# An adaLN block with attention and a mixture of experts: sums of the shared weights prepared in the last batch, the second norm's centring on another engine, other buffers for the experts

## The chip, the cores and the metric

The kernel runs on one core of one Trainium2 chip. The metric is device time in microseconds (us) of one execution. The core's engines are PE (TensorE, matrix products), DVE (VectorE), ACT (ScalarE), POOL (GpSimd) and SP (SyncE, which here issues nearly all DMA transfers). Each engine works through its own list of instructions in order and waits on semaphores that other engines or transfers raise.

## The reference, cut to what matters

All data are float32. x has 4 batches of 512 tokens of width 512. The six modulation rows come from c.

```python
mod = (silu(c) @ wmod).reshape(4, 6, 1, -1)
sa, ca, ga, sb, cb, gb = (mod[:, i] for i in range(6))      # ga, gb kept away from 0
h = layernorm(x) * (1 + ca) + sa
x = x + ga * attention(h)          # 16 heads of 128, causal softmax, q/k/v/o with biases
h = layernorm(x) * (1 + cb) + sb
x = x + gb * ffn(h)
```

ffn is a mixture of 8 experts (SwiGLU, 352 wide, the best 2 of 8 by a softmax over `gate_weight`) plus a shared SwiGLU MLP of width 704 over all tokens:

```python
g = silu(x @ w_gate[e].T) * (x @ w_up[e].T)          # routed, weighted by the two best scores
y = sum_e cw[:, e] * (g @ w_down[e].T)
y = y + (silu(x @ sw_gate.T) * (x @ sw_up.T)) @ sw_down.T
```

## The kernel before

**Products of seven.** Large matrix products are cut into 2 x 2 quadrants and made with seven products instead of eight (`seven`, L483). Each operand then needs seven slots: its four quadrants, partly overwritten, and sums of them. `sums_of_a` (L466) and `sums_of_b` (L473) make the sums in four operations of one engine, over the slots of one tile. For the q, k, v and o weights, the sums made in batch 0 are stored to DRAM tensors (`sums`, L141) and loaded in the later batches.

**Attention.** Batch b (B = 4) has four groups of four heads; G counts the sixteen groups, u the heads of a group (loop at L1018). For a head, `first_half` makes the scores: PE products into `ps`, DVE mask L756 and maximum L758, ACT's exponential L760. `second_half` makes the rest a head later: DVE's reciprocal L764, ACT's scaling of prob in four pieces L767, PE's transposes `ppt` L777, the copies to `probT` by DVE (L785) or ACT (L787), PE's `po` L791 and ACT's `oS` L798. The sums of oS are made on POOL (L468 to L471). The projections of other groups fill in between: `weave_at` takes steps of the fill (next_k, next_v, next_o, with products w_k L612, w_v L660, w_o L697) by the tables PLANS, OPENING and LAST, written by hand. `second_norm(b - 1)` (L916) is a side generator, stepped at fixed spots of batch b's first two groups.

**The second norm** is `normed(b, 2)` (L207). For each of four blocks of 128 tokens, DVE multiplies the attention output by ga (L217) and POOL adds x (L218). DVE takes mean and variance (L223, L224), L228 adds epsilon, and ACT makes rstd by Ln and Exp (L229, L230). After a yield, DVE makes xh = (x - mean) * rstd (L233) for each block, multiplies by 1 + cb (L242), and POOL adds sb (L243). PE turns xh (`pln`, L251); then `route` (L274) computes the experts' scores, picks two (`hit`, L351) and counts tokens ahead of each (`prk`, L357 and L360), from which come the slots to which POOL scatters the tokens (L380).

**The shared weights.** `wshr` holds, one after the other, five chunks of gate and up weights (ws, each four quadrants of 2 x 128 columns), the tail wst, and the down weights sdn (four quadrants of 3 x 256). At the second head of the last group, (G, u) = (15, 1), the pool of attention's weights is closed and the tiles ws[0] to ws[4] and wst are opened (L1059). wst, ws[0] and ws[1] are loaded there; at (15, 3) DVE makes the sums of those two (L1083). After attention SP loads h2s of batches 0 and 1 (L1470), the other three ws and sdn. POOL makes the sums of h2s_0, ws[2] to ws[4] and sdn, and DVE those of h2s_1 (L1495 to L1500).

**After attention.** `shared(0)` makes the hidden layer of the shared MLP for batches 0 and 1, five chunks of seven products each (`shared_hidden` L1169, matmul w_s L1177, DVE L1189 to L1207, SiLU on ACT L1190 and L1194, the product into hid L1218), then the down products (w_d L1250) with the sums of hid on DVE or POOL (L1235). `shared_tail` (L1148, pst L1152) makes the narrow tail chunk. Between its steps runs `slots_found` (L1502): the second norm of batch 3, its route and the plan of tiles. Then come 39 tiles of 128 tokens for the experts (loop at L1534) with two buffers each for the weights wgu and wdn; at tile 4 h2s of batches 2 and 3 are loaded. Last comes `half2`: shared(2) for batches 2 and 3, woven (L1577 to L1579) with `combined`, which fetches the experts' outputs by indirect DMA, scales and adds them (L1459 to L1465) and writes the output. In `half2` POOL makes the sums of h2s_2 and DVE those of h2s_3.

**Memory and order.** The pool `moe` (L1114) opens when attention's pool closes, and takes over its memory: gb_bc, sdn, then wgu[0], wgu[1], wdn[0], wdn[1], then two h2s tiles. A tile there waits for the former users of the memory under it. The order on PE, DVE, ACT and SP is as the program writes it (`manual_schedule`); POOL's order is chosen by a scheduler from its dependencies.

Of the kernel before, what the change touches and what calls it, by code (L numbers as in the profile page):

```python
# [8 lines left out]
F32 = mybir.dt.float32  # L9
# [5 lines left out]
P = 128  # L15
# [15 lines left out]
SQ = 4 * 2 * P  # L31
FK = 3
FL = FS // 2 - 2 * P
SW = NSC * SQ + NC * P + 4 * FK * HW
EGU = 2 * NC * F
TOPK = 2
# [11 lines left out]
def adaln_block_kernel(  # L48
# [29 lines left out]
    def bank(tag, name):  # L78
        if tag in ("ps", "pt"):
            return psum.tile([P, 512], F32, tag=tag, name=name)  # L80
        bufs = {"w": 3, "po": 1}[tag]
        return psum2.tile([P, 512], F32, tag=tag, bufs=bufs, name=name)
# [30 lines left out]
    for i in range(NT):  # L113
# [29 lines left out]
        "wk": dram.tile([H // 2, P, 5 * 2 * DH], F32, name="sums_k"),  # L143
        "wv": dram.tile([NG, P, 5 * 4 * DH], F32, name="sums_v"),
        "wo": dram.tile([NG, P, 2 * 6 * HW], F32, name="sums_o"),
    }


# [58 lines left out]
    def normed(b, n, fine=(1,)):  # L207


        if n == 1:  # L210
            src = xh = late["first"]
        else:
            src = xres[b]
            xh = late["x"]
            rows = late["mod"]
            for t in range(NTB):
                nc.vector.tensor_mul(src[:, t, :], src[:, t, :], ga_bc)  # L217
                nc.gpsimd.tensor_add(src[:, t, :], src[:, t, :], xh[:, t, :])  # L218
                yield
        mv = small.tile([P, NTB, 2], F32, tag="mv", name=f"mv_{n}_{b}")  # L220
        for t in range(NTB):
            st = small.tile([P, 6], F32, tag="st", name=f"st_{n}_{b}_{t}")
            nc.vector.bn_stats(st, src[:, t, :])  # L223
            nc.vector.bn_aggr(mv[:, t, :], st)  # L224
            if t in fine:
                yield
        rstd = small.tile([P, NTB], F32, tag="rstd", name=f"rstd_{n}_{b}")
        nc.vector.tensor_scalar_add(rstd, mv[:, :, 1], EPS)  # L228
        nc.scalar.activation(rstd, rstd, AF.Ln)  # L229
        nc.scalar.activation(rstd, rstd, AF.Exp, scale=-0.5)  # L230
        yield
        for t in range(NTB):
            nc.vector.tensor_scalar(  # L233
                xh[:, t, :],
                src[:, t, :],
                mv[:, t, 0:1],
                rstd[:, t : t + 1],
                op0=ALU.subtract,
                op1=ALU.mult,
            )  # L240
            if n == 2:
                nc.vector.tensor_mul(xh[:, t, :], xh[:, t, :], rows[0])  # L242
                nc.gpsimd.tensor_add(xh[:, t, :], xh[:, t, :], rows[1])  # L243
            if t in fine:
                yield
        late[b] = xh
# [27 lines left out]
    def route(b, xh):  # L274
# [77 lines left out]
        for t in range(NTB):  # L352
            k = b * NTB + t
            nc.vector.tensor_add(seen[:, k + 1, :], seen[:, k, :], hit[:, t, :])
        yield
        pr = bank("pt", f"prk_{b}")[:, : NTB * NE]
        nc.tensor.matmul(  # L357
            pr, lhsT=before, rhs=hit.rearrange("p t e -> p (t e)"), start=True, stop=False
# [114 lines left out]
    def sums_of_b(eng, w):  # L473

        eng.tensor_sub(w[:, 4], w[:, 3], w[:, 1])
        eng.tensor_sub(w[:, 1], w[:, 1], w[:, 0])
        eng.tensor_sub(w[:, 5], w[:, 3], w[:, 1])
        eng.tensor_sub(w[:, 6], w[:, 5], w[:, 2])

    att = left.enter_context(tc.tile_pool(name="att", bufs=2))  # L480
    wts = right.enter_context(tc.tile_pool(name="wts", bufs=2, side="right"))
# [434 lines left out]
    def second_norm(b):  # L916
# [2 lines left out]
        yield  # L919
        yield from route(b, late[b])  # L920


    def by_turns(*gens):

# [77 lines left out]
    with tc.manual_schedule(engines={ENG.PE, ENG.DVE, ENG.Activation, ENG.SP}):  # L1002
# [11 lines left out]
        weave(queries(0), 8 * SEVEN, fill, 18)  # L1014
        drain(fill)

        pending = None
        for G in range(NGB):  # L1018
            b, g = divmod(G, NG)

# [12 lines left out]
            for u in range(GH):  # L1033
                prob = att.tile([P, 10 * P], F32, tag="prob", name=f"prob_{G}_{u}")
                parts = [first_half(G, u, prob)]
                if pending is not None:
                    parts.append(second_half(*pending))
                pending = (G, u, prob)


                spots = ()
                if g == 0 and b > 0 and u > 0:
                    if u == 1:
                        second = side = second_norm(b - 1)
# [12 lines left out]
                next(parts[0])  # L1057
                weave_at(main, plans[u], fill, side if spots else None, spots)
                if (G, u) == (NGB - 1, 1):  # L1059
                    right.close()  # L1060
                    shp = right.enter_context(
                        tc.tile_pool(name="shared", bufs=1, side="right")
                    )
                    ws = [
                        shp.tile([P, 7, 2, P], F32, tag=f"ws{k}", name=f"ws{k}")
                        for k in range(NSC)
                    ]
                    wst = shp.tile([P, NC, P], F32, name="wst")
                    nc.sync.dma_start(
                        out=wst.rearrange("p c n -> p (c n)"),  # L1070
                        in_=wshr[:, NSC * SQ : NSC * SQ + NC * P],
                    )

                    def load_ws(k):
                        nc.sync.dma_start(
                            out=ws[k][:, :4].rearrange("p q c n -> p (q c n)"),
                            in_=wshr[:, k * SQ : (k + 1) * SQ],
                        )

                    load_ws(0)  # L1080
                    load_ws(1)
                if (G, u) == (NGB - 1, 3):
                    sums_of_a(nc.vector, ws[0])  # L1083
                    sums_of_a(nc.vector, ws[1])
                if g == 3 and u == 3 and b + 1 < B:

                    long = in_order(second_half(*pending), next_v(G + 1))
                    weave(queries(b + 1), 8 * SEVEN, long, 4 + SEVEN)
                    pending = None

                if b + 1 < B:
                    if (g, u) == (2, 0):
                        load_first(b + 1)
                if (g, u) == (0, 1):
                    wos[G] = load_wo(b, 0)
                if (g, u) == (0, 2 if b > 0 else 1):
                    open_out(b)
                if (g, u) == (3, 2):
                    load_for_second(b)

                k, n = GH * G + u - 1, NROW // P // NFILL
                if 0 <= k < NFILL:
                    nc.sync.dma_start(
                        out=xs[k * n * P : (k + 1) * n * P, :].rearrange(
                            "(p n) (c w) -> p (n c) w", p=P, w=P
                        ),
                        in_=nothing.unsqueeze(1).to_broadcast([P, n * NC, P]),
                    )
# [9 lines left out]
    h2s, hids = {}, {}  # L1118
    phase = []

    wgu = [moe.tile([P, EGU], F32, tag=f"wgu{j}", bufs=1, name=f"wgu{j}") for j in range(2)]
    wdn = [moe.tile([P, EW - EGU], F32, tag=f"wdn{j}", bufs=1, name=f"wdn{j}") for j in range(2)]

    def load_h2(b):
        h2s[b] = moe.tile([P, 7, 2, HW], F32, tag="h2", name=f"h2s_{b}")
        nc.sync.dma_start(
            out=h2s[b][:, :4].rearrange("p q c n -> p (q c n)"),
            in_=h2[b].rearrange("p q c n -> p (q c n)"),
        )

    def flat_of(a):
        return a.rearrange("p q c n -> p (q c n)")
# [336 lines left out]
    with tc.manual_schedule(engines={ENG.PE, ENG.DVE, ENG.Activation, ENG.SP}):  # L1469
        load_h2(0)  # L1470
        load_h2(1)
        for k in range(2, NSC):
            load_ws(k)
        nc.sync.dma_start(
            out=flat_of(sdn[:, :4]), in_=wshr[:, NSC * SQ + NC * P :]
        )
        spread(gb_bc, GB)

        def load_xr(b, pool, tag):
# [15 lines left out]
        sums_of_b(nc.gpsimd, h2s[0])  # L1495
        shared_tail(1)
        sums_of_b(nc.vector, h2s[1])
        for k in range(2, NSC):
            sums_of_a(nc.gpsimd, ws[k])
        sums_of_b(nc.gpsimd, sdn)  # L1500

        def slots_found():  # L1502
            yield from in_order(normed(B - 1, 2, (0, 1, 2)))
# [30 lines left out]
        for i in range(NT + 1):  # L1534
# [15 lines left out]
            if i == 4:  # L1550
                load_h2(2)
                load_h2(3)


        open_phase("half2")
# [2 lines left out]
        load_xr(2, moe, "xr0")  # L1558
        load_xr(0, moe, "xr1")
        shared_tail(2)  # L1560
        sums_of_b(nc.gpsimd, h2s[2])
        shared_tail(3)
        sums_of_b(nc.vector, h2s[3])
        for m in range(4):
            fetch(m, order[m])

# [8 lines left out]

        main, fill = shared(2), combined()
        weave(main, 4, iter(()), 0)  # L1577
        weave(main, NSEV - 4, fill, 6 * NTB)
        weave(main, 2 * SEVEN + 1, fill, 2 * NTB)  # L1579
        drain(main)  # L1580
        drain(fill)
        parts.close()
# [111 lines left out]
```

## Time and profile before

| what | us |
| --- | --- |
| median of 3 runs (lowest, highest) | 1825.65 (1824.71, 1828.13) |
| the profiled execution | 1824.61 |
| its span, first to last instruction | 1822.9 |
| PE busy in the span | 1735.1 |
| DVE, ACT, POOL busy | 897.9, 551.0, 616.8 |
| attention ends (last w_o product done) | 1248 |
| shared(0) ends, tiles begin | 1381 |
| tiles end, half2 begins | 1701 |
| last matmul done | 1811.5 |

The profiled execution is one run; its span leaves 1.7 us of its time outside. In a timeline, a row is a run of like instructions: start, duration, engine, line, operation, operands (out<-in), shape, count; brackets at the end hold the idle time of that engine just before and the instruction that ended it. The granted clock is the share of full speed that TensorE's throttle allowed; 1 is full speed, 0.5 half. PE is busy except for some 88 us, 25 of them before 45 us and after 1811 us, while the first data come in and the last go out.

### The profile page before, as it was taken

How to read it: one execution, taken by the hardware profiler on the slowest of the kernel's cores; microseconds unless marked ns; L12 is line 12 of the kernel's file. 1: busy time of each engine (PE TensorE's matmuls, PEld its weight loads, DVE VectorE, ACT ScalarE, POOL GpSimd, SP SyncE). 2: the span in 40 equal slices, each digit the busy share in tenths (PEclk: the TensorE clock that was granted, in tenths of full speed). 3: DMA queues.
4: the chain of work that ended last, by engine and by line, in shares of the span. 5: the costliest groups of instructions: out<-in, count | busy, mean ns of one | idle time of the engine just before them, and what ended most of it. 6: DMA issues, size and time to landing. Idle time of an engine off the chain costs nothing.

```text
span 1822.9 us, 21901 instructions
## 1 busy us (share of the span) xinstructions
PE 1735.1 (95%) x7637; PEld 1321.2 (72%) x7637; DVE 897.9 (49%) x1884; ACT 551.0 (30%) x1325; POOL 616.8 (34%) x702
## 2 busy tenths in 40 slices
PE   6999999998999999899999899998899999999997
PEld 4767777786887788688788678875686556556685
DVE  4554454457545555654555655444673111211486
ACT  1034444214445412544430444441300111111220
POOL 6334662305243303352320425336341000000575
PEclk9999999999999999999999999999999999999999
DMA  6569899645343333442343243225042656453442
GB/s 247 177 199 294 267 305 312 197 160 193 107 138 113 116 127 113 159 143 88 122 142 108 104 121 127 81 68 203 24 170 88 238 174 220 167 192 132 147 143 75
DMA packets 145007, 287.25 MB, mean 158 GB/s; under 512 B 8177, under 2 KB 86513, under 8 KB 138241
## 3 DMA queue, kind: packets, MB, share of 16 engines
q1 hardware_dynamic: 139776, 269.07, 44.2%
q0 software_dynamic: 5120, 16.78, 2.8%
q8 instruction: 61, 1.00, 0.2%
q14 instruction: 50, 0.40, 0.1%
HBM read 247.38 MB, written 89.69 MB: 185 GB/s over the span
## 4 chain that ended last, share of the span: by engine, by line
PE 77%; DVE 8%; POOL 5%; DMA 4%; ACT 3%; issue 2%; SPq 0%; POOLq 0%; DVEq 0%; ACTq 0%
PE w_v L660 10%; PE w_o L697 10%; PE w_q L574 10%; PE w_k L612 7%; PE ps L749 6%; PE po L791 6%; PE pyt L1419 5%; PE pgt L1392 5%; PE put L1392 5%; PE w_s L1177 3%; PE w_d L1250 3%; PE ppt L777 3%; ACT prob L767 1%; DVE xh L242 1%; PE pxt L1379 1%
## 5 line engine op out<-in xcount | busy, mean ns | idle before, releaser
L760 ACT ACTIVATE prob<-ps,nmax 128x128 f32<-128x128 f32 (+3 forms) x256 | 134.2, 525 | 362.0 <-DVE nmax L758 362.0
L612 PE MATMUL w_k<-h,wk 128*128 128x256 f32 x896 | 222.6, 387 | 4.5 <-ACT p_k L624 2.7
L660 PE MATMUL w_v<-wv,h 128*128 128x256 f32 x896 | 206.1, 380 | 3.0 <-DVE kT L627 1.8
L697 PE MATMUL w_o<-wo,oS 128*128 128x256 f32 x896 | 209.0, 380 | 0.0
L574 PE MATMUL w_q<-h,wq 128*128 128x256 f32 x896 | 203.6, 382 | 1.4 <-DVE qT L600 1.4
L574 PEld LDWEIGHTS w_q<-h,wq 128*128 128x128 f32 x896 | 170.1, 192 | 27.7 <-issue 3.4
L660 PEld LDWEIGHTS w_v<-wv,h 128*128 128x128 f32 x896 | 167.6, 190 | 24.7 <-DVE kT L627 2.2
L612 PEld LDWEIGHTS w_k<-h,wk 128*128 128x128 f32 x896 | 165.8, 195 | 26.8 <-ACT p_k L624 5.8
L697 PEld LDWEIGHTS w_o<-wo,oS 128*128 128x128 f32 x896 | 164.9, 191 | 21.0 <-issue 1.4
L749 PE MATMUL ps<-kT,qT 128*128 128x128 f32 (+3 forms) x512 | 173.5, 440 | 1.7 <-ACT prob L760 1.4
L791 PE MATMUL po<-probT,v 128*128 128x512 f32 (+3 forms) x512 | 150.9, 436 | 11.4 <-DVE probT L785 11.4
L791 PEld LDWEIGHTS po<-probT,v 128*128 128x128 f32 x512 | 95.2, 190 | 68.6 <-issue 28.9
L777 PEld LDWEIGHTS ppt<-ident,prob 128*128 128x128 f32 x640 | 82.9, 142 | 81.9 <-issue 35.9
L767 ACT ACTIVATE prob<-prob,rsum 128x128 f32<-128x128 f32 (+3 forms) x256 | 122.8, 551 | 61.2 <-DVE rsum L764 61.2
L710 POOL TENSOR_TENSOR xres<-xres,p_o 128x512 f32<-128x512 f32 x48 | 60.9, 1269 | 231.0 <-DVE xres L710 137.1
L1177 PE MATMUL w_s<-h2s,ws 128*128 128x256 f32 x560 | 127.6, 386 | 8.8 <-DVE wgu L1207 3.0
L758 DVE TENSOR_REDUCE nmax<-ps 128x1 f32<-128x128 f32 (+3 forms) x256 | 125.8, 491 | 8.8
L1177 PEld LDWEIGHTS w_s<-h2s,ws 128*128 128x128 f32 x560 | 106.1, 192 | 28.4 <-DVE wgu L1207 3.6
L777 PE MATMUL ppt<-ident,prob 128*128 128x128 f32 x640 | 109.2, 278 | 14.9 <-ACT prob L767 12.3
L1419 PE MATMUL pyt<-wdn,hTt 128*128 128x512 f32 (+1 forms) x234 | 107.0, 593 | 0.6 <-ACT yt L1427 0.6
L756 DVE TENSOR_TENSOR ps<-ps,cmask 128x128 f32<-128x128 f32 x256 | 75.0, 293 | 59.9 <-PE ps L749 51.5
L1402 DVE TENSOR_TENSOR ht<-tsg,put 128x352 f32<-128x352 f32 x39 | 20.3, 521 | 170.4 <-PE put L1392 165.7
(270 smaller groups left out, 2433.9 us busy)
## 6 DMA issues: line engine op xcount, KB each, us to landing
wgu<-in_wexp_dram SPq DMA_DIRECT2D x39, 1408.0 KB
xs<-nothing SPq DMA_DIRECT2D x15, 2304.0 KB, 15.6
wdn<-in_wexp_dram SPq DMA_DIRECT2D x39, 768.0 KB, 4.7
wo<-sums_o SPq DMA_DIRECT2D x12, 1536.0 KB, 8.3
wq<-sums_q SPq DMA_DIRECT2D x24, 640.0 KB, 4.6
wk<-sums_k SPq DMA_DIRECT2D x24, 640.0 KB, 4.7
wv<-sums_v SPq DMA_DIRECT2D x12, 1280.0 KB, 7.6
xt<-xs SPq DMA_DIRECT2D x39, 256.0 KB, 3.6
```

What stands on the lines that cost most here:

```text
L574: nc.tensor.matmul(dst, lhsT=w[:, sa, c, :], rhs=h7[b][:, sb_, c, :], start=c == 0, stop=c == 1,)
L612: nc.tensor.matmul(dst, lhsT=w[:, sa, c, :], rhs=h7[b][:, sb_, c, :], start=c == 0, stop=c == 1,)
L660: nc.tensor.matmul(dst[:, t2 * HW : (t2 + 1) * HW], lhsT=h7[b][:, sb_, c, t2 * P : (t2 + 1) * P], rhs=w[:, sa, c, :], start=t2 == 0 and c ...
L697: nc.tensor.matmul(dst[:, t2 * HW : (t2 + 1) * HW], lhsT=oSs[hp][:, sa, t2 * P : (t2 + 1) * P], rhs=w[:, hp, sb_, :], start=t2 == 0 and hp ...
L749: nc.tensor.matmul(ps[:, :n], lhsT=qT[:, q0 : q0 + P], rhs=kT[:, u % 2, :n], start=True, stop=True,)
L760: nc.scalar.activation(blk, ps[:, :n], AF.Exp, bias=nmax, accum_out=rsum[:, i : i + 1])
L767: nc.scalar.mul(blk, blk, rsum[:, k : k + 1])
L777: nc.tensor.transpose(pt[:, at : at + P], prob[:, QO[i] + j * P : QO[i] + (j + 1) * P], ident,)
L791: nc.tensor.matmul(po[:, j * P :], lhsT=v()[:, j, u * DH : (u + 1) * DH], rhs=probT[:, KO[j] : KO[j] + (NTB - j) * P], start=(j == 0), sto ...
L1177: nc.tensor.matmul(dst[:, n * HW : (n + 1) * HW], lhsT=ws[k][:, sa, c, :], rhs=h2s[b + n][:, sb_, c, :], start=(n == 0 and c == 0), stop=( ...
L1392: nc.tensor.matmul(ps[:, :F], lhsT=xT[:, c, :], rhs=wgu[i % 2][:, at : at + F], start=(c == 0), stop=(c == NC - 1),)
L1419: nc.tensor.matmul(py, lhsT=hT_t[:fn, k, :], rhs=wdn[i % 2][:fn, k * D : (k + 1) * D], start=(k == 0), stop=(k == len(FCH) - 1),)
```

## The change

1. A generator `shared_sums` is stepped after each of the first twelve heads of the last batch's groups 0 to 2. It loads one chunk of ws into a buffer of the former wq weights, has POOL make its sums, and at its next step stores all seven slots to a new DRAM tensor, five times; then the same for sdn in four pieces of 64 columns. The host lays sdn out by these pieces.
2. At (15, 1) all five ws are loaded from there, whole, and after attention the whole of sdn. The sums at (15, 3) and those of ws and sdn after attention are gone.
3. In the second norm, of all four batches, ACT makes xh as Identity(x * rstd + less), and a new DVE operation behind Exp makes less = -mean * rstd.
4. In `route` of the last batch there is one more yield ahead of prk.
5. In `moe`, wdn comes first, then both h2s tiles, then wgu.
6. Of the sums of h2s_2 and h2s_3, three each are made by POOL at tile 8, the fourth by POOL after the shared tails; DVE makes none of them.
7. The weave of half2 is cut differently: four steps alone, 29 with 24 steps of the combination, five alone, 12 with 8 (before: 4 alone, 31 with 24, 15 with 8).

```diff
+    "ws": dram.tile([NSC, P, 7, 2, P], F32, name="sums_s"),
+    "sdn": dram.tile([P, 7, FK, HW], F32, name="sums_d"),
...
         nc.scalar.activation(rstd, rstd, AF.Exp, scale=-0.5)
+        if n == 2:
+            less = small.tile([P, NTB], F32, tag="less", name=f"less_{n}_{b}")
+            nc.vector.scalar_tensor_tensor(
+                less, mv[:, :, 0], -1.0, rstd, op0=ALU.mult, op1=ALU.mult
+            )
         yield
         for t in range(NTB):
-            nc.vector.tensor_scalar(
-                xh[:, t, :], src[:, t, :], mv[:, t, 0:1], rstd[:, t : t + 1],
-                op0=ALU.subtract, op1=ALU.mult,
-            )
-            if n == 2:
+            if n == 1:
+                nc.vector.tensor_scalar(...)
+            else:
+                nc.scalar.activation(
+                    xh[:, t, :], src[:, t, :], AF.Identity,
+                    bias=less[:, t : t + 1], scale=rstd[:, t : t + 1],
+                )
                 nc.vector.tensor_mul(xh[:, t, :], xh[:, t, :], rows[0])
                 nc.gpsimd.tensor_add(xh[:, t, :], xh[:, t, :], rows[1])
...
         yield
+        if b == B - 1:
+            yield
         pr = bank("pt", f"prk_{b}")[:, : NTB * NE]
...
+    def shared_sums():
+        n = HW // ND
+        for k in range(NSC):
+            w = wts.tile([P, 7, 2, P], F32, tag="wq", name=f"ws_sums_{k}")
+            nc.sync.dma_start(
+                out=w[:, :4].rearrange("p q c n -> p (q c n)"),
+                in_=wshr[:, k * SQ : (k + 1) * SQ],
+            )
+            sums_of_a(nc.gpsimd, w)
+            yield
+            nc.sync.dma_start(out=sums["ws"][k], in_=w)
+        for k in range(ND):
...
+            sums_of_b(nc.gpsimd, w.rearrange("p (q c n) -> p q c n", q=7, c=FK))
+            yield
+            dst = sums["sdn"].rearrange("p q c n -> p (q c) n")
+            nc.sync.dma_start(out=dst[:, :, k * n : (k + 1) * n], in_=w.rearrange("p (q n) -> p q n", n=n))
+        yield
...
-                    load_ws(0)
-                    load_ws(1)
-                if (G, u) == (NGB - 1, 3):
-                    sums_of_a(nc.vector, ws[0])
-                    sums_of_a(nc.vector, ws[1])
+                    for k in range(NSC):
+                        nc.sync.dma_start(out=ws[k], in_=sums["ws"][k])
...
+                if b == B - 1 and g < 3:
+                    next(prepare, None)
...
+    wdn = [moe.tile([P, EW - EGU], F32, tag=f"wdn{j}", bufs=1, name=f"wdn{j}") for j in range(2)]
+    for b in range(half):
+        h2s[b] = moe.tile([P, 7, 2, HW], F32, tag="h2", name=f"h2s_{b}")
     wgu = [moe.tile([P, EGU], F32, tag=f"wgu{j}", bufs=1, name=f"wgu{j}") for j in range(2)]
-    wdn = [moe.tile([P, EW - EGU], F32, tag=f"wdn{j}", bufs=1, name=f"wdn{j}") for j in range(2)]
...
-        for k in range(2, NSC):
-            load_ws(k)
-        nc.sync.dma_start(out=flat_of(sdn[:, :4]), in_=wshr[:, NSC * SQ + NC * P :])
+        nc.sync.dma_start(out=sdn, in_=sums["sdn"])
...
-        for k in range(2, NSC):
-            sums_of_a(nc.gpsimd, ws[k])
-        sums_of_b(nc.gpsimd, sdn)
...
+            if i == 8:
+                most_of_b(nc.gpsimd, h2s[2])
+                most_of_b(nc.gpsimd, h2s[3])
...
-        sums_of_b(nc.gpsimd, h2s[2])
         shared_tail(3)
-        sums_of_b(nc.vector, h2s[3])
+        rest_of_b(nc.gpsimd, h2s[2])
+        rest_of_b(nc.gpsimd, h2s[3])
...
-        weave(main, NSEV - 4, fill, 6 * NTB)
-        weave(main, 2 * SEVEN + 1, fill, 2 * NTB)
+        weave(main, NSEV - 6, fill, 6 * NTB)
+        weave(main, 5, iter(()), 0)
+        weave(main, 2 * SEVEN - 2, fill, 2 * NTB)
```

`most_of_b` makes slots 4, 5 and 6 of `sums_of_b` (with slot 5 from slots 4 and 0), `rest_of_b` the new slot 1.

More of the change, by code (lines that the diff above doesn't have):

```diff
@@ L33 @@
 FL = FS // 2 - 2 * P
+ND = 4
 SW = NSC * SQ + NC * P + 4 * FK * HW
@@ L230, in normed @@
         nc.scalar.activation(rstd, rstd, AF.Exp, scale=-0.5)
+        if n == 2:
[3 more added lines that the diff above has]
+            )
         yield
         for t in range(NTB):
[L233 to L239, printed above, removed]
-            )
-            if n == 2:
+            if n == 1:
+                nc.vector.tensor_scalar(
+                    xh[:, t, :],
+                    src[:, t, :],
+                    mv[:, t, 0:1],
+                    rstd[:, t : t + 1],
+                    op0=ALU.subtract,
+                    op1=ALU.mult,
+                )
+            else:
+                nc.scalar.activation(
+                    xh[:, t, :],
+                    src[:, t, :],
+                    AF.Identity,
+                    bias=less[:, t : t + 1],
+                    scale=rstd[:, t : t + 1],
+                )
                 nc.vector.tensor_mul(xh[:, t, :], xh[:, t, :], rows[0])
@@ L478, in sums_of_b, with most_of_b, rest_of_b @@
         eng.tensor_sub(w[:, 6], w[:, 5], w[:, 2])
+    def most_of_b(eng, w):
+        eng.tensor_sub(w[:, 4], w[:, 3], w[:, 1])
+        eng.tensor_add(w[:, 5], w[:, 4], w[:, 0])
+        eng.tensor_sub(w[:, 6], w[:, 5], w[:, 2])
+    def rest_of_b(eng, w):
+        eng.tensor_sub(w[:, 1], w[:, 1], w[:, 0])
     att = left.enter_context(tc.tile_pool(name="att", bufs=2))
@@ L920, in second_norm @@
         yield from route(b, late[b])
+    def shared_sums():
[5 more added lines that the diff above has]
+                in_=wshr[:, k * SQ : (k + 1) * SQ],
+            )
+            sums_of_a(nc.gpsimd, w)
+            yield
+            nc.sync.dma_start(out=sums["ws"][k], in_=w)
+        for k in range(ND):
+            w = wts.tile([P, 7 * 2 * P], F32, tag="wq", name=f"sdn_sums_{k}")
+            at = NSC * SQ + NC * P + k * 4 * FK * n
+            nc.sync.dma_start(
+                out=w[:, : 4 * FK * n], in_=wshr[:, at : at + 4 * FK * n]
+            )
+            w = w[:, : 7 * FK * n]
+            sums_of_b(nc.gpsimd, w.rearrange("p (q c n) -> p q c n", q=7, c=FK))
[3 more added lines that the diff above has]
+        yield
     def by_turns(*gens):
@@ L1015, in adaln_block_kernel @@
         drain(fill)
-        pending = None
+        pending, prepare = None, shared_sums()
         for G in range(NGB):
@@ L1072, in adaln_block_kernel @@
                     )
[L1074 to L1078, printed above, removed]
-                    load_ws(0)
-                    load_ws(1)
-                if (G, u) == (NGB - 1, 3):
-                    sums_of_a(nc.vector, ws[0])
-                    sums_of_a(nc.vector, ws[1])
+                    for k in range(NSC):
+                        nc.sync.dma_start(out=ws[k], in_=sums["ws"][k])
                 if g == 3 and u == 3 and b + 1 < B:
@@ L1119, in adaln_block_kernel @@
     phase = []
+    wdn = [moe.tile([P, EW - EGU], F32, tag=f"wdn{j}", bufs=1, name=f"wdn{j}") for j in range(2)]
+    for b in range(half):
+        h2s[b] = moe.tile([P, 7, 2, HW], F32, tag="h2", name=f"h2s_{b}")
     wgu = [moe.tile([P, EGU], F32, tag=f"wgu{j}", bufs=1, name=f"wgu{j}") for j in range(2)]
-    wdn = [moe.tile([P, EW - EGU], F32, tag=f"wdn{j}", bufs=1, name=f"wdn{j}") for j in range(2)]
     def load_h2(b):
-        h2s[b] = moe.tile([P, 7, 2, HW], F32, tag="h2", name=f"h2s_{b}")
+        if b not in h2s:
+            h2s[b] = moe.tile([P, 7, 2, HW], F32, tag="h2", name=f"h2s_{b}")
         nc.sync.dma_start(
@@ L1471, in adaln_block_kernel @@
         load_h2(1)
-        for k in range(2, NSC):
-            load_ws(k)
-        nc.sync.dma_start(
-            out=flat_of(sdn[:, :4]), in_=wshr[:, NSC * SQ + NC * P :]
-        )
+        nc.sync.dma_start(out=sdn, in_=sums["sdn"])
         spread(gb_bc, GB)
@@ L1628, in downs_by_quadrant @@
                 q[k, c, p : p + n] = w[n0 : n0 + n].reshape(n, 2, HW)
-        return q.transpose(2, 0, 3, 1, 4).reshape(P, 4 * FK * HW)
+        q = q.transpose(2, 0, 3, 1, 4).reshape(P, 4 * FK, ND, HW // ND)
+        return q.transpose(0, 2, 1, 3).reshape(P, 4 * FK * HW)
     wk_h = a["attn_Wk"].reshape(D, H, DH)
```

## The prediction

> **What bounds the kernel now.** The page's first part comes first: PE is busy for nearly the whole span, so only what stops PE, or slows it, moves the end.
>
> ```profile
> PE 1735.1 (95%) x7637; PEld 1321.2 (72%) x7637; DVE 897.9 (49%) x1884; ACT 551.0 (30%) x1325; POOL 616.8 (34%) x702
> ```
>
> The list of PE's waits over the span then says what stops it (microseconds in total, times, longest):
>
> ```profile
> PE ppt L777 <- ACT prob L767: 12.3, 18, 2.1
> PE po L791 <- DVE probT L785: 11.4, 8, 3.0
> PE pst L1152 <- DMA h2s<-h: 5.4, 1, 5.4
> ```
>
> To see where these waits lie I read PE's timeline, first at the end of attention and in shared(0); the brackets hold the idle time ahead of a row and its releaser:
>
> ```profile
> 1248.07 3.60 PE L1152 MATMUL pst<-h2s,wst 128*128 128x512 f32 x8
> 1257.08 5.06 PE L1152 MATMUL pst<-h2s,wst 128*128 128x512 f32 x8 [5.41 <-DMA h2s<-h]
> ...
> 1281.57 1.99 PE L1177 MATMUL w_s<-h2s,ws 128*128 128x256 f32 x8 [3.03 <-DVE wgu L1207]
> ...
> 1323.82 0.41 PE L357 MATMUL prk<-hit,before 128*128 128x32 f32 x2 [2.61 <-DVE hit L351]
> ```
>
> The same eight matmuls take 3.60 without a wait and 5.06 after one: the idle time costs a stretch at half clock too (granted clock 0.76 from 1255 to 1262). SP's and POOL's timelines there say why:
>
> ```profile
> 1228.34 23.95 SPq L1126 DMA_DIRECT2D h2s<-h  x2
> ```
>
> ```profile
> 1278.74 1.26 POOL L218 TENSOR_TENSOR xres<-xres,xh 128x512 f32<-128x512 f32 x1
> ```
>
> One row holds both h2s loads: the first went out at 1228.34, the second 23.6 us later, since its buffer had u_o, p_o and xres of the last output product as former users. POOL sums ws and sdn from 1259 on and comes to the norm's add at 1278.74; DVE's bn_stats waits 3.61 for it, and L1207, for which PE waits, is queued behind bn_stats.
>
> The third place is the second norm of batch 0 inside batch 1's attention (batches 1 and 2 repeat it at 738 and 1038 to 0.1 us). DVE, ACT, then PE:
>
> ```profile
> 436.80 0.17 DVE L228 TENSOR_SCALAR rstd<-mv 128x4 f32<-128x4 f32 x1
> ...
> 437.81 0.55 DVE L785 COPY probT<-ppt 128x384 f32<-128x384 f32 x1
> 438.96 0.55 DVE L233 TENSOR_SCALAR xh<-xres,mv,rstd 128x512 f32<-128x512 f32 x1 [0.61 <-ACT rstd L230]
> ```
>
> ```profile
> 438.72 0.21 ACT L230 ACTIVATE rstd<-rstd 128x4 f32<-128x4 f32 x1
> ```
>
> ```profile
> 438.41 0.92 PE L791 MATMUL po<-probT,v 128*128 128x256 f32 x4 [1.54 <-DVE probT L785]
> ...
> 443.35 0.73 PE L777 MATMUL ppt<-ident,prob 128*128 128x128 f32 x2 [2.14 <-ACT prob L767]
> ...
> 448.49 0.33 PE L251 MATMUL pln<-ident,xh 128*128 128x128 f32 x1 [0.82 <-POOL xh L243]
> ```
>
> While ACT loads two tables and makes rstd (to 438.93), DVE does three operations of attention (the mask at 436.88, nmax at 437.20, the copy to probT at 437.81); the last of them frees PE at 438.41.
>
> The last place is half2, where DVE is behind:
>
> ```profile
> 1775.80 2.00 PE L1250 MATMUL w_d<-sdn,hid 128*128 128x256 f32 x8 [2.21 <-DVE hid L1218]
> ...
> 1787.82 2.87 PE L1250 MATMUL w_d<-sdn,hid 128*128 128x256 f32 x12 [1.69 <-DVE h2s L1310]
> ```
>
> **A, end of attention and shared(0): −15.5.** With wdn and the two h2s tiles laid out first, the second h2s load follows the first at once (about 1228.9) and lands near 1245, before PE wants it at 1251.7. That removes 5.41, the half clock (5.06 − 3.60 = 1.46) and some 0.26 of matmul tail that a stop exposes: 7.1. The eight DVE sums of ws (1229.8 to 1233.0) go; probT L785 stood behind them and PE waited 0.33, then; about 0.4. The 16 POOL sums of ws and sdn (1259 to 1281.8) go, so the norm's adds come at about 1261 to 1267 instead of 1278.7 to 1285.4. The seven waits of w_s from 1267.78 to 1296.62 (1.32, 0.33, 3.03, 1.00, 1.07, 0.36, 1.00 = 8.11, and 7 × 0.26 of tail) make 9.9. In their place come four: 0.6 for the h2s sums, 1.45 where L1189 is held behind the new `less` (L228 started at 1287.38 and Exp ended at 1289.30, so DVE stands for 1.75), 1.3 and 0.7 where L1202 and its like stand behind multiplies that now wait for ACT's xh, a third table load (1.28) and a SiLU (0.63). Net 7.1 + 0.4 + 9.9 − 4.05 = 13.4. The extra yield puts prk one product (1.73) later: 2.61 becomes about 1.1, and the half clock after it (24 matmuls in 7.11 instead of 5.2 to 5.4, about 1.7) goes: 3.2. The planning after it is a step later too and costs about 1 at the end of the stage (PE waits 0.60 at 1342.96 today). 13.4 + 3.2 − 1.0 = 15.6, taken as 15.5; 11 to 18 by whether the new four cost double or half, and whether prk's half clock stays.
>
> The whole ws, five times 917 KB instead of two times 512, are asked for at 1203; by the best slice of the page's row (312 GB/s) that takes 14.7 us, to 1218, ahead of the wo load at 1223.6. sdn (2.75 MB) is wanted only at 1344. Both cost nothing; a wo that came late by some us would cost as much.
>
> The Trainium skill, page "TensorE: Matmul & The Clock Gate", section "HAM oscillation — how this bites in real kernels", warns of PE gaps over some 3.4 us; prk's 2.8 would then cost no clock, and A would be 1.7 less. The rows above have half clock after such gaps, and the rows decide.
>
> **B, half2: −4.4.** The four DVE sums of h2s_3 (1710.4 to 1713.3) go, and PE has no wait there, so that is worth nothing; the six sums moved to the eighth tile lie where POOL is idle and PE runs without a stop (0 to 0.5 if POOL slowed DVE). What counts is the weave: no combine for five steps at the end of the hidden products. By DVE's order one combine (0.74 to 0.96, and 0.69) is done before and two come after L1360's group. hid moves from 1775.75 to 1773.75, the releaser of the second wait from 1787.8 to 1783.4. Of the three waits (0.64, 2.21, 1.69: 4.54, and tails) some 0.85 stays. 2 to 5. The tail after the last matmul (1811.5 to 1822.9) stays.
>
> **C, the second norm on ACT, three times in attention: +12.6.** `less` stands in DVE's order right after L228 and waits for Exp. Queued behind it are the mask, nmax and probT, and PE waits for the last. `less` itself is a 128x4 operation like L228 (0.17). So probT ends at 440.5 and po starts at 440.6 instead of 438.41: +2.16. ACT makes xh by Identity, which the trace has with a scale and bias as oS L798, 0.67 and without a table load among Exps. After the late nmax and u_k, ACT ends xh of t0 and t1 at 442.4; DVE multiplies them (0.69, or 1.63 beside POOL) and only then makes the reciprocal at 443.2 to 444.1 (442.69 before). The four scalings (1.92) end at 445.2 to 446.1, oS at 445.8 to 446.7. POOL's order has now the four oS sums (0.73, up to 1.0) ahead of xh t2 and t3 (1.26 each): the last xh is there at 451.2 to 452.3, and pln goes on 2.8 to 3.8 later than at 448.49. This contains the shift of po. PE has then stood for about 4 us, and a half-clock stretch of 3.4 us costs up to 1.7, of which the first stretch today (444.1, four w_k in 1.91 instead of 1.03) pays 0.9. Per batch 2.8 to 5.5; I take 4.2, thrice. From below: DVE is relieved of four L233 (0.51 to 0.95), and were the stall hidden, no more than pln's 0.82 could be won, so 0 to 1.3 is the low end.
>
> **D, the sums in the last batch: +1.** 20 POOL operations of 128x256 (0.73) and 16 of 128x192 (0.55 by size, between 0.3 and 1.17) make about 23.4 us, spread over nine steps of about 24 us. POOL's idle time hides them (it stood 8.9 us before u_k at 440.09). Each store is issued a step after its sums, so SP should not stand at it; its 18 more issues take 0.35 to 0.6 each, ahead of loads that are issued 10 us or more before use. 0 to 4. The stores of sdn come in runs of 256 bytes, 10,752 in all; at the mean packet time of the page (44.2% of 16 engines' span over 139,776 packets: 92 ns) they take 62 us of 16 engines over four steps, which nothing waits for. The Trainium skill, page "DMA: Bandwidth & Descriptors", section "Specifications", says that transfers under 512 bytes become read-modify-write; no row here shows it, and even doubled they would be done 30 us before the sdn load.
>
> **Sum.** The profiled execution took 1824.6 (span 1822.9 and 1.7 around it). 1824.6 − 15.5 − 4.4 + 12.6 + 1.0 = 1818.3. The median of the runs shown is 1825.65, 1.0 longer, so the forecast of a median is **1819.3**. 0.2% (3.65 us) is about what a measurement tells from no change.
>
> **Rivals.** (1) *The norm costs little*: the steps behind `less` have slack that I don't see, C is 2. For it: PE waits for ACT's prob right after in any case (2.14). Against: PE waited for probT to the very end of its copy. 1824.6 − 15.5 − 4.4 + 2 + 1, and 1.0: 1808.7. Chance 0.20. (2) *The gains are eaten*: in shared(0) the norm's new waits cost double and prk's clock stays (A 12), B is 2.5: 1825.65 − 12 − 2.5 + 12.6 + 1: 1824.8, no change. That the change doesn't do what it says is of this kind: were the second h2s load held as now, 7.1 less would give 1826.4. Chance 0.22. (3) *Slower*: SP holds in the last batch. Each of nine stores stands in SP's order ahead of wk, wv and wo loads; if POOL comes late to a sum (behind u_k and oS additions that wait for DVE), the load behind it is late and PE stops. A stop of 2 us with its half clock (1.7) is 3.7; it decides from three of them on (11.1 give 1830.4, past the 1829.3 where slower begins); four give 1834.1. For it: SP already stood 35.6 us once for PE, so its order does hold. Against: a store has a whole step's slack. C at its upper end (16) needs only two. Chance 0.16. The forecast, 1815 to 1822, has 0.42.
>
> **Range.** From 1807.5, which takes in rival 1, to 1830, which leaves out most of rival 3. Faster 0.62, within 0.2% 0.22, slower 0.16.
>
> **What would show it.** A: pst without a wait, w_s waits of about 4 in all, prk's wait near 1. B: about 0.85 of waits from 1770 on. C: po's wait at the norms about 3.7 instead of 1.54, pln's 3 to 4 instead of 0.82, `less` released by ACT. D: no new wait on wk, wv, wo. It is wrong if pln's wait stays under 1 (then rival 1), or if the last batch's steps are longer than those of batch 2.

## The result and the profile after

The changed kernel takes 1826.5 us (median of 12 runs, 1824.51 to 1831.47), the kernel before 1826.87 beside it (12 runs). The ratio is 0.9997, with a 95% interval of 0.9987 to 1.0008: no difference that can be measured, where 6.3 us less were forecast (1819.3 from 1825.65). The profiled execution of the changed kernel, 1831.47, is the longest of its twelve, 5.0 above their median. So the places below are read by their own lengths, and totals by the timed runs.

Here is the first part of the page of the changed kernel. PE is busy 6.6 us longer at the same number of matmuls. That goes with the clock, not with work: the mean granted clock is 0.983 in this execution and 0.990 in the one before.

```profile
PE 1741.7 (95%) x7637; PEld 1326.9 (73%) x7637; DVE 884.8 (48%) x1860; ACT 562.7 (31%) x1341; POOL 628.3 (34%) x726
```

In the list of PE's waits after, pst and L1257 (L1207 before) are gone. po has grown from 11.4, pln from 2.6, and L1254 (L1204 before) from 1.0:

```profile
PE po L818 <- DVE probT L812: 18.6, 8, 4.0
PE pln L267 <- POOL xh L259: 15.2, 6, 4.3
...
PE w_s L1227 <- DVE wgu L1254: 2.6, 1, 2.6
```

Where the time goes is seen best by taking the 7637 matmuls of both programs in order and subtracting their starts. The shift of the changed kernel against before, in us:

| place (time of before) | shift | change since the row above |
| --- | --- | --- |
| ahead of the first second norm (423) | +2.4 | +2.4, two more half-clock stretches at 269 among it |
| behind the norms of batches 0, 1, 2 (460, 764, 1059) | +10.2, +15.3, +19.8 | +7.8, +5.1, +4.5 |
| last batch, beside its new sums (1088, 1119) | +20.6, +22.5 | +0.8, +1.9 |
| end of attention (1235) | +21.8 | −0.7 |
| shared(0), behind prk (1328) | +6.6 | −15.2 |
| end of shared(0) (1380) | +7.4 | +0.8 |
| end of the tiles (1700) | +7.8 | +0.4 |
| half2, behind its last wait (1789) | +6.9 | −0.9 |

The norms' 17.4 in this execution is more than the timed runs give below; at the same places run 1, which leaves the norm on DVE, shifts by 2.5.

The end of attention and shared(0) gain about what was forecast. In PE's timeline there, all sixteen pst matmuls run in one go, and the waits of w_s and prk are short.

```profile
1269.89 7.03 PE L1202 MATMUL pst<-h2s,wst 128*128 128x512 f32 x16
...
1302.35 3.90 PE L1227 MATMUL w_s<-h2s,ws 128*128 128x256 f32 x16 [1.18 <-DVE wgu L1252]
...
1333.95 0.41 PE L375 MATMUL prk<-hit,before 128*128 128x32 f32 x2 [0.69 <-DVE hit L367]
```

Next comes the norm of batch 0 after, DVE first: `less` stands 1.99 for ACT's rstd, with the mask, nmax and probT behind it.

```profile
441.36 0.17 DVE L236 SCALAR_TENSOR_TENSOR less<-mv,rstd 128x4 f32<-128x4 f32 x1 [1.99 <-ACT rstd L233]
...
442.37 0.55 DVE L812 COPY probT<-ppt 128x384 f32<-128x384 f32 x1
```

POOL takes the four sums of oS ahead of the last two adds of xh; before, the first of these sums began at 448.39, behind all four adds:

```profile
448.45 0.73 POOL L486 TENSOR_TENSOR oS<-oS 128x256 f32<-128x256 f32 x1 [0.34 <-ACT oS L825]
...
451.59 0.72 POOL L489 TENSOR_TENSOR oS<-oS 128x256 f32<-128x256 f32 x1
452.27 2.48 POOL L259 TENSOR_TENSOR xh<-xh,rows 128x512 f32<-128x512 f32 x2
```

So PE waits at po for 3.70 instead of 1.54, and at pln for 4.33 and 0.89 instead of 0.82:

```profile
442.97 1.11 PE L818 MATMUL po<-probT,v 128*128 128x256 f32 x4 [3.70 <-DVE probT L812]
...
453.59 0.33 PE L267 MATMUL pln<-ident,xh 128*128 128x128 f32 x1 [4.33 <-POOL xh L259]
454.81 0.47 PE L267 MATMUL pln<-ident,xh 128*128 128x128 f32 x1 [0.89 <-POOL xh L259]
```

In half2 the waits of 2.21 and 1.69 are gone, and others stand ahead of them, where PE had run 34.5 us without a stop before (from 1734.72):

```profile
1765.29 11.21 PE L1227 MATMUL w_s<-h2s,ws 128*128 128x256 f32 x48 [0.50 <-DVE wgu L1256]
1779.10 1.99 PE L1227 MATMUL w_s<-h2s,ws 128*128 128x256 f32 x8 [2.60 <-DVE wgu L1254]
```

What DVE does ahead of L1254 takes longer there. Between two L1204 of the kernel before (1753.36 and 1766.52) lie 13.2 us, with two combinations, the product into hid and the four sums of hid among others; between two L1254 after (1761.12 and 1778.36) lie 17.2 us, with three combinations and the same others. The product into hid, before and then after:

```profile
1758.74 1.87 DVE L1218 TENSOR_TENSOR hid<-wgu,wgu 128x1024 f32<-128x1024 f32 x1 [0.70 <-ACT wgu L1194]
```

```profile
1769.18 2.46 DVE L1268 TENSOR_TENSOR hid<-wgu,wgu 128x1024 f32<-128x1024 f32 x1 [0.70 <-ACT wgu L1244]
...
1778.36 0.68 DVE L1254 TENSOR_TENSOR wgu<-w_s,wgu 128x512 f32<-128x512 f32 x1
```

In the last batch, POOL's timeline at the first piece of sdn shows the four new sums between the adds of xres; the sums of oS, two more adds and u_k come after them:

```profile
1126.59 0.60 POOL L493 TENSOR_TENSOR sdn_sums<-sdn_sums 128x192 f32<-128x192 f32 x1
...
1130.82 0.60 POOL L496 TENSOR_TENSOR sdn_sums<-sdn_sums 128x192 f32<-128x192 f32 x1
...
1138.15 0.72 POOL L658 TENSOR_TENSOR u_k<-u_k,u_k 128x256 f32<-128x256 f32 x1
```

DVE's kT waits for that u_k (2.24 before), and probT is behind kT:

```profile
1138.90 0.42 DVE L654 SCALAR_TENSOR_TENSOR kT<-w_k,u_k 128x256 f32<-128x256 f32 x1 [4.42 <-POOL u_k L658]
...
1140.18 0.55 DVE L812 COPY probT<-ppt 128x384 f32<-128x384 f32 x1
```

### The profile page after: what moved, and what is told of

It is laid out like the page before. It is cut to its first block, busy times and chain, and to the rows that moved or that the text cites. A ratio compares the mean times of both kernels' runs of the same rounds, so it can differ in the third digit from the quotient of the medians.

```text
span 1829.8 us, 21973 instructions
## 1 busy us (share of the span) xinstructions
PE 1741.7 (95%) x7637; PEld 1326.9 (73%) x7637; DVE 884.8 (48%) x1860; ACT 562.7 (31%) x1341; POOL 628.3 (34%) x726
## 4 chain that ended last, share of the span: by engine, by line
PE 79%; DVE 7%; POOL 5%; ACT 3%; DMA 3%; issue 2%; SPq 0%; POOLq 0%; ACTq 0%; DVEq 0%
PE w_v L687 10%; PE w_q L601 10%; PE w_o L724 9%; PE w_k L639 7%; PE ps L776 6%; PE po L818 6%; PE pyt L1469 5%; PE pgt L1442 5%; PE put L1442 5%; PE w_s L1227 4%; PE w_d L1300 4%; PE ppt L804 3%; ACT prob L794 1%; PE pxt L1429 1%; DMA xt<-xs 1%
```

## The experiments

The theory after the traces was this: the gain of about 16 us (0.7 and 15.2) from the end of attention to behind prk is real; the three norms give back some 13, the sums in the last batch 3, and the new weave of half2 brings next to nothing. Its rivals were that the norms cost little in a typical execution, or that the sums in the last batch are the large loss. Times are medians; ratios are to the kernel before, run beside them. By the intervals, the difference between two rows is uncertain by 3 to 4 us.

| run | us | ratio, 95% interval |
| --- | --- | --- |
| the change | 1826.5 | 0.9997, 0.9987 to 1.0008 |
| 1: change, norm on DVE | 1813.6 | 0.9925, 0.9909 to 0.9941 |
| 2: before, norm on ACT | 1841.2 | 1.0074, 1.0058 to 1.0090 |
| 3: change, old weave | 1828.1 | 1.0002, 0.9989 to 1.0016 |
| 4: change, less later | 1825.5 | 0.9987, 0.9976 to 0.9999 |
| 5: before, new buffers | 1825.7 | 0.9993, 0.9983 to 1.0004 |
| 6: before, sums in the last batch | 1820.8 | 0.9971, 0.9961 to 0.9982 |
| 7: as 4, xh ahead of oS | 1814.8 | 0.9936, 0.9923 to 0.9950 |
| 8: as 1, two gaps in the sums | 1809.4 | 0.9903, 0.9888 to 0.9918 |
| 9: as 8, combinations later | 1809.1 | 0.9908, 0.9892 to 0.9923 |
| 10: as 8, no extra yield | 1816.6 | 0.9936, 0.9920 to 0.9953 |

**1, the change with the norm as before.**

```diff
-        if n == 2:
-            less = ...
...
-            if n == 1:
-                nc.vector.tensor_scalar(...)
-            else:
-                nc.scalar.activation(xh[:, t, :], src[:, t, :], AF.Identity, ...)
+            nc.vector.tensor_scalar(xh[:, t, :], src[:, t, :], ...)
+            if n == 2:
```

> The change with the second norm left as it was (xh on DVE, no less), in all four batches. Theory (the gain at the end of attention is real, about 16 us, and the three norms inside attention give it back, about 4.5 us each and clock on top): 13 to 19 us faster than before, some 1808 to 1813 in terms of before's 1826. Rival one (the norms cost little; the gain in shared(0) was never there in a typical execution): within 3 us of before. Rival two (the sums in the last batch give it back, as late loads and late probT there): 2 to 5 us faster than before, no more. In the profile: po's wait at the three norms 1.54 again, pln's below 1.

It is 13.7 us faster than before, and 0.9925 / 0.9997 puts it 13.2 below the change. In its trace po waits 1.53 at the first norm and pln 0.81, as expected. The theory holds; both rivals fall, since neither leaves room for 13 us.

**2, the norm alone on ACT, in the kernel before** (the same edit the other way).

> The kernel before with only the second norm on ACT. Theory: 13 to 20 us slower than before (three times 4.5, some clock, and up to 4 in shared(0) where DVE stands at less behind two table loads). Rivals one and two: 0 to 4 us slower. In the profile: po waits 3.7 at each of the three norms, pln 4 or more.

It is 0.74% slower, 13.5 us. What 1 gains, 2 loses, so within the uncertainty the norm's cost adds to the other parts and doesn't depend on them. The profiled execution is 8.6 above its median; it shifts by 7.8, 5.1 and 4.3 at the three norms, and by 4.7 from there into the tiles, some of it in half-clock stretches at 1253 and 1407.

**3, the change with half2's weave of before.**

```diff
-        weave(main, NSEV - 6, fill, 6 * NTB)
-        weave(main, 5, iter(()), 0)
-        weave(main, 2 * SEVEN - 2, fill, 2 * NTB)
+        weave(main, NSEV - 4, fill, 6 * NTB)
+        weave(main, 2 * SEVEN + 1, fill, 2 * NTB)
```

> The change with the weave of half2 as before (4, 31 with 24, 15 with 8). The prediction's term B: 4.4 us slower than the change (the two waits of 2.21 and 1.69 come back). Theory now, from the traces of before and after: the new weave takes these two waits away and makes one of 2.6 in the last chunk of the hidden products, so the old weave is 0 to 1.5 us slower, hard to tell from no difference.

It can't be told from the change (0.05% apart, well inside the intervals). The forecast's 4.4 is excluded, or nearly so: 0.24% would put the ratio at 1.0021, above this interval. In its trace the first of the two waits is back at 2.22, the second only at 0.6; half2 moves by −0.2 against before, where the change has −0.9.

**4, less behind the yield.**

```diff
         nc.scalar.activation(rstd, rstd, AF.Exp, scale=-0.5)
+        yield
         if n == 2:
             less = ...
-        yield
```

> The change with less made after the yield, so that mask, nmax and probT stand ahead of it in DVE's order. If DVE's stand at less is what costs (the prediction's first step of C): po's wait at the norms is 1.5 again, pln goes on some 2.2 us earlier per norm, and with 1 to 2 in shared(0) the run is 6 to 10 us faster than the change. If the order on POOL (four sums of oS ahead of the last two adds of xh) and ACT's place in the chain cost more: po's wait is 1.5 but pln's stays at 4 or more, and the run gains less than 4.

It gains 1.8 us by the ratios, which is not clear of nothing. PE's timeline shows why no more: po is back at 1.54, and pln waits as long as ever.

```profile
440.25 0.92 PE L818 MATMUL po<-probT,v 128*128 128x256 f32 x4 [1.54 <-DVE probT L812]
...
451.77 0.33 PE L267 MATMUL pln<-ident,xh 128*128 128x128 f32 x1 [4.34 <-POOL xh L259]
```

So DVE's stand at less was the smaller part.

**7, as 4, with all four blocks of xh in one step for batches 0 to 2**, so that all four stand ahead of oS on POOL, and ahead of prob's scaling on ACT and of the reciprocal on DVE; the number of steps is kept.

```diff
-            if t in fine:
+            if t in fine and (n == 1 or len(fine) > 1):
                 yield
+        if n == 2 and len(fine) == 1:
+            yield
```

> The run with less made later, and with all four blocks' xh in one step in batches 0 to 2, so that POOL has its four adds of xh ahead of the four sums of oS. If that order on POOL is the larger part of the norm's cost (theory now): pln goes on at about 4 us less after ppt, its wait falls from 4.3 to below 2, and the run is 6 to 11 us faster than with less later alone (about 1816). If ACT's place in the chain is what costs: pln still waits 3 or more, ppt waits longer, and the run gains less than 3.

0.9936 against 0.9987 makes it 9.3 us faster than 4. PE now waits earlier, at ppt, since DVE multiplies four blocks ahead of the reciprocal, and pln follows without a wait.

```profile
447.69 2.00 PE L806 MATMUL ppt<-ident,prob 128*128 128x128 f32 x4 [3.86 <-ACT prob L796]
...
451.19 1.03 PE L269 MATMUL pln<-ident,xh 128*128 128x128 f32 x4
```

So the late step of the last two blocks is the larger part of the norm's price. Run 7 moves it on three engines at once, and no run moves it on POOL alone. Run 4's trace gives an estimate of POOL's share: DVE had multiplied both blocks by 449.10, yet POOL, busy with the sums of oS, began their adds at 450.45 and ended them at 452.94; with POOL free, the last add (1.27) could have ended at about 450.4. That is some 2.5 per norm, 7.5 of the 9.3, without what it changes in clock. With the blocks grouped, ACT is about as good as DVE for this step (0.9936 and 0.9925).

**5, the kernel before with the new buffers alone** (wdn, both h2s tiles, then wgu).

> The kernel before with only the new order of buffers in moe (wdn, both h2s tiles, wgu). By the prediction's working, the wait of 5.41 at pst goes with its half clock: 7.1. Theory: that alone can't be kept whole, because POOL still has the sums of ws and sdn ahead of the norm's adds, so that PE, now earlier, waits longer at the products released by L1207: 2 to 6 us faster than before. Rival (the terms simply add): 7 faster.

It is 1.1 us faster, below the lower end of what was expected, and hardly to be told from nothing. In PE's timeline pst runs through, then the time is lost at L1211 (L1207 before), 6.18 instead of 3.03.

```profile
1249.98 7.03 PE L1156 MATMUL pst<-h2s,wst 128*128 128x512 f32 x16
...
1281.36 8.86 PE L1181 MATMUL w_s<-h2s,ws 128*128 128x256 f32 x32 [6.18 <-DVE wgu L1211]
```

POOL's timeline has the norm's first add where it was before (1278.74 then): POOL's work didn't come earlier with PE's.

```profile
1278.52 1.26 POOL L218 TENSOR_TENSOR xres<-xres,xh 128x512 f32<-128x512 f32 x1
```

**6, the kernel before with the sums in the last batch alone** (parts 1 and 2 of the change).

> The kernel before with only the sums of ws and sdn in the last batch, and their loads whole. Theory: the waits of w_s in shared(0) go (9.9 in the prediction's working, with DVE's norm a little less of it replaced), attention's last batch loses 2.9 at the two places that the change shows (late v at 1087, late probT at 1118 in the time of before): 5 to 8 us faster than before; pst's wait stays. Rival (the last batch's sums take back what they give): within 2 of before.

It is 6.0 us faster, as expected. The trace loses 0.6 and 2.0 in the last batch and gains 8.8 from there to behind prk; pst's wait stays:

```profile
1261.13 5.97 PE L1175 MATMUL pst<-h2s,wst 128*128 128x512 f32 x8 [5.32 <-DMA h2s<-h]
```

Buffers (1.1) and sums (6.0) make 7.1 apart. With both, and the yield (6.0 us by runs 8 and 10), that is 13.1; run 1 has 13.7.

**8, as 1, without sums after two heads of the last batch.**

```diff
-                if b == B - 1 and g < 3:
+                if b == B - 1 and g < 3 and (g, u) not in ((1, 1), (2, 1)):
                     next(prepare, None)
```

> The change with the second norm on DVE, and with no sums after the second head of the groups 1 and 2 of the last batch (the first and the last piece of sdn come one and two heads later). Theory: the late probT (1.7 and tail) at that place came from these four POOL sums standing ahead of oS, xres and u_k, so it goes: 1.5 to 2.5 us faster than the change with the norm on DVE, if the piece does not make the same wait a head later. Rival (it is POOL's or the queue's load as such): no change.

It is 4.0 us faster than 1 by the ratios, more than expected, though the uncertainty covers what was expected. In the traces 2.0 lies at the place meant, where po now has no wait (1.75 in run 1), and 1.0 in half2, where run 1's execution has a half-clock stretch (1761, 3.4 us) and this one has none. The rest is not explained.

```profile
1120.45 2.32 PE L805 MATMUL po<-probT,v 128*128 128x512 f32 x8
```

This version and 9 are the fastest of all: 0.97% below before.

**9, as 8, with the combinations moved back.**

```diff
-        weave(main, NSEV - 6, fill, 6 * NTB)
-        weave(main, 5, iter(()), 0)
-        weave(main, 2 * SEVEN - 2, fill, 2 * NTB)
+        weave(main, NSEV - 10, fill, 20)
+        weave(main, 9, iter(()), 0)
+        weave(main, 2 * SEVEN - 2, fill, 12)
```

> The run with the norm on DVE and the gaps, and half2's weave cut again: 25 steps with 20 of the combination, nine alone, 12 with 12. No combination then stands in DVE's order between the last chunk's first product and the four sums of hid. If the 2.6 wait of w_s for L1254 of the change (the new wait that ate B) comes from DVE being a combination or two behind there, it goes, and the run is 2 to 3.5 us faster than with the gaps alone (about 1806.5). Rival: the combinations moved back come out again behind the last matmul or as waits of w_d for h2s, and nothing is won (within 1 of 1809.4).

No difference from 8 shows, as the rival said; the uncertainty leaves room for the 2 us at the theory's lower end. The trace shows where the gain goes. PE's timeline has no stop any more from 1739.72 to the last matmul at 1789.6, and its lead over 8 grows from 2.8 us ahead of half2 to 8.3 behind the hidden products.

```profile
1739.72 13.54 PE L1214 MATMUL w_s<-h2s,ws 128*128 128x256 f32 x62
```

But the table of windows (length, then busy time and instructions of PE, PE's loads, DVE, ACT, POOL, clock, DMA share, GB/s) shows 7.4 us of DVE behind the last matmul, where 8 has 2.7, each in its own window:

```profile
1790.00:1806.00 16.00, 0.00 (x0) 0.00 (x0) 7.44 (x8) 0.00 (x0) 5.83 (x4) 0.56 0.23 82
```

```profile
1798.00:1810.00 12.00, 0.00 (x0) 0.00 (x0) 2.74 (x4) 0.00 (x0) 3.05 (x3) 0.69 0.19 66
```

From the last matmul to the end of the span it takes 15.5 us instead of 11.5: of the 5.5 that PE gains in half2, 4.0 come back as a longer end.

**10, as 8, without the extra yield.**

```diff
-        if b == B - 1:
-            yield
         pr = bank("pt", f"prk_{b}")[:, : NTB * NE]
```

> The run with the norm on DVE and the gaps, without the extra yield in route of the last batch. By the prediction's working the yield is worth the wait at prk and its half clock (3.2): 3 us slower than with the gaps. Rival: with the norm's adds early the scores are early too, so prk would not wait long anyway: 0 to 1 slower.

0.9936 against 0.9903 makes it 6.0 us slower, give or take 4; in the pair of traces 4.3 lie in shared(0). The wait is the one of before, 2.60, and the 24 matmuls behind it take 8.43; in run 8 the wait is 0.67 and they take 5.43.

```profile
1314.08 0.41 PE L360 MATMUL prk<-hit,before 128*128 128x32 f32 x2 [2.60 <-DVE hit L354]
...
1315.13 8.43 PE L1212 MATMUL w_s<-h2s,ws 128*128 128x256 f32 x24
```

```profile
1313.85 0.41 PE L362 MATMUL prk<-hit,before 128*128 128x32 f32 x2 [0.67 <-DVE hit L354]
...
1314.69 5.43 PE L1214 MATMUL w_s<-h2s,ws 128*128 128x256 f32 x24
```

## Why the prediction was wrong

The forecast was 1819.3, the measured time is 1826.5, 7.2 more. Of these, 1.2 is the kernel before, which took 1826.87 beside the change and 1825.65 in the runs that the forecast started from. The change itself was forecast at −6.3 and measured at −0.4, so 5.9 is to be explained. Term by term:

- **A, −15.5: right.** The traces give −15.9 from the end of attention to behind prk, where the working has −16.6, and 0.8 back at the end of shared(0), where it has 1.0: −15.1. prk waits 0.69 (1.1 forecast). Two sizes inside were off and nearly cancel: the norm's own waits in shared(0) were put at 3.45 and cost about 1.1 (run 1, without them, gains 17.0 to behind prk), and the other terms, 20.0 by the working, were too high by 3. What the working didn't say, and run 5 shows, is that the 7.1 at pst could only be kept because POOL's sums went too.
- **C, +12.6: right.** The norm costs 13.2 (run 1) or 13.5 (run 2) in all, and about 1.1 of that lies in shared(0), so some 12 in attention. Both steps are seen: probT 2.16 later at po, and POOL's order at pln. Their shares were not foreseen: putting `less` later brings 1.8 us (run 4), putting the last two blocks earlier 9.3 (run 7).
- **B, −4.4: the step that failed.** It was "Of the three waits (0.64, 2.21, 1.69: 4.54, and tails) some 0.85 stays". The two large ones did go, and yet half2 moves by −0.9 in the change's trace and +0.2 in run 1's, and run 3 finds no difference. The stops of half2 come to 3.74 after (0.50, 2.60, 0.64) instead of 4.54. The working began at the waits and looked only behind them. Ahead of 1769 PE had no wait before, but little slack: with 24 steps of the combination in 29 instead of 31, one more combination stands in DVE's order ahead of L1254, multiplies take longer beside POOL (L1268: 2.46 instead of 1.87), and w_s waits 2.60 and 0.50. Run 9 points the same way: with these waits gone, DVE's work came out behind the last matmul. It must be done before the end, and a weave chooses where it is waited for.
- **D, +1: too small, though within its bounds.** It is 2.7 in the change, 2.7 in run 1 and 2.6 in run 6. The cover named was POOL's idle time; at one step POOL was not idle, and oS, xres and u_k queued behind four sums of 0.6. Run 8 takes 2.0 back. The other 0.8 lies at 1088: POOL begins v 0.7 later, behind a sum of ws, and DVE's `seen` additions (L370), now beside POOL's next one, take 1.77 instead of 0.77. SP did stand at the new stores, for 18 us together, without making a load late enough to stop PE: rival 3 did not occur.

Against the forecast, A is off by 0.4, C by −0.5, B by 3.5 and D by 1.7; 0.4 more came in the tiles, where PE waited 0.40 at 1589 for a second load of xt (why it came later is not shown). That is 5.5 of the 5.9, added up from single traces and from ratios that are uncertain by some us, so that it fits so well is partly luck.

Rival 2, "the gains are eaten", gave 1824.8 and had 0.22. Its time is nearly right, and of its reasons one: B fell short, by more than it said. Shared(0) kept its gain.

## What to carry to other kernels

A wait is not a sum that can be collected by itself. Before counting it as won, look for the next engine that is late at the same place (run 5), and for the work of the late engine that must still be done before the end (run 9). When an operation moves to another engine, look at the order that this makes on a third: here POOL, ordered by a scheduler, put other sums ahead, and by the estimate at run 7 that cost more than the new wait at `less`. Grouping the operations (run 7) or leaving them where they were (run 1) was worth 0.5 to 0.7%. Idle time of an engine covers added work only step by step: compare the added operations with the queue of the very step into which they go.

## What the runs showed of the hardware

In the traces the half clock comes, while PE still has work, in stretches of 3.4, 6.8, 10.2 or 13.7 us, and how many follow the same stop differs from one execution to the next. At the norm of batch 0 on DVE, with po's wait at 1.53 or 1.54 in both, it began at 444.1 and lasted 3.4 in the kernel before; in run 1 it began at 440.4 and lasted 13.7, for 1.9 us more of shift. At prk, stops of 2.6 and 0.2 were followed by 3.4 in the kernel before and by 6.8 in run 10, where the 24 matmuls behind took 7.11 and 8.43 instead of 5.43. In half2, a stop of 2.60 to 2.62 was followed by 3.4 at half clock in runs 1, 7 and 10, and by none in the change and in run 8. So what a stop costs in clock can't be read from one execution: the extra yield, forecast at 3.2, is worth 4.3 by a pair of traces and 6.0, give or take 4, by the timed runs.

The Trainium skill, page "TensorE: Matmul & The Clock Gate", section "HAM oscillation — how this bites in real kernels", has PE gaps over some 3.4 us as what slows the clock; stops of 2.6 and 0.2 us did it here. The length that the section "What's actually happening" of that page gives for the free-running window, 3413 ns, fits the steps of 3.4.

The stores of sdn, in runs of 256 bytes, took 7.1 us for 672 KB in the change (median), 95 KB a us, and those of ws 6.0 us for 896 KB, 149 KB a us. The stores of sdn were not slower in every run: in run 8 they took 5.3 us and those of ws 7.1, 127 and 126 KB a us. Either is half or less of the 15 us for each store of sdn that the working had allowed.
